# A selective scan on four engines: the state ring, the decays' lead and the order of the sums

## The chip, the cores and the metric

The kernel runs on one core of a Trainium2 chip. The core has five engines with an instruction queue each: PE (TensorE, matrix products), DVE (VectorE) and POOL (GpSimd) for elementwise work, ACT (ScalarE) for functions such as exp, and SP, which here only issues DMAs. The queues run side by side; an instruction that needs another engine's result waits for a semaphore, and everything behind it in its own queue waits with it. The metric is the device time of one execution in microseconds (us); lower is better.

## What is computed

Four sequences of 256 tokens with 512 features pass through two layers. The first is a layer norm with latent attention and a gated feed-forward beside it. The second is a layer norm with a selective state space block and a routed low-rank feed-forward beside it. The change concerns the state space block. Its core, cut from the reference:

```python
proj = hidden_states @ in_proj_w
x, z = jnp.split(proj, 2, axis=-1)
...
xc = jax.nn.silu(xc)                    
ssm_p = jnp.einsum('bdl,ed->ble', xc, x_proj_w)
...
def step(h, inp):
    x_t, dt_t, B_t, C_t = inp
    dA = jnp.exp(dt_t[..., None] * A)
    dBx = dt_t[..., None] * B_t[:, None, :] * x_t[..., None]
    h = dA * h + dBx
    y = jnp.einsum('bdn,bn->bd', h, C_t)
    return (h, y)
...
y = (ys + D_param[None, :, None] * xc) * jax.nn.silu(z)
return jnp.einsum('bdl,hd->blh', y, out_proj_w)
```

There are 1024 channels (d) and 16 states (n) for each of the four sequences (b), and the recurrence runs over 256 steps. All data is float32.

## The kernel before

The order of all work is written out by hand: each engine's queue holds its instructions in the order in which the program calls the helpers.

**Units.** The scan is cut into 128 units u = 0 to 127. Each sequence (called batch here) has PER = 32 of them: 8 columns c of 128 channels, each with NU = 4 groups g of four states. Unit u belongs to batch u // 32, column u % 32 // 4 and group u % 4. In a unit's tile of 128 x 1024 elements, the partitions hold 32 channels for each of four states, and the row holds four blocks of 256 time steps.

A unit passes through these steps:

- *spread* (line 937), once a column: four DMAs on SP each bring dt and dt*x of the column into the unit layout, as dts and dus (two tiles each).
- *decays* (971): four exponentials on ACT, line 982, exp(dt * A), into a decay tile. The first column of each block stays 0, so that one scan runs over all four blocks. From unit 4 on there are three decay tiles, used in turn.
- *scan_in* (986): from unit 8 on a no-op on DVE (989) that takes over two waits of what follows, for the decays of u and for the product with C of u-2. Then bx = B * (dt*x) into a PSUM tile on DVE (993).
- *scan* (998): the recurrence h = decay * h + bx along the row on DVE (1008), into one of two h tiles, and then the product hc = h * C on POOL (1013), into one of three hc tiles. Units 0 to 3 take tiles that other work lends (the table `lent`).
- *states_sum* (1019): four small matmuls on PE (1025) with the matrix `stack` add the four states of each channel into the PSUM tile ysum, over the four units of a column. For the first group a matmul with a diagonal matrix (1023) goes ahead: it starts ysum with D * x.
- *take_sum* (1028): ACT copies ysum away when a column is done (1030). The next column's line 1023 has to wait for that.

**The loop over units** (1384) issues, pass by pass: take_sum of a column whose last unit was u-2; decays of u+2; the work that the tables put here; scan_in(u); scan(u); gates; states_sum(u-1). The tables `at`, `mid_at`, `late_at` and `end_at` hold all else, by batch and unit: while batch b is scanned, the layer norm of batch b+1, its input projection (px, pz), its convolution (conv_in, conv_taps; dg, tap and xc on ACT, products with px on PE, some sums on POOL), its silu (conv_silu, unit 16 or 17), the projection to dt, B and C (pp_mm, units 17 and 18) and the step sizes (step_in, step_exp, step_out, step_x, from unit 21 on) are made, and the output of batch b-1 (out_mm, dense, expert_out). In the last batch only output remains beside the scan.

The first units also overlap the end of the first layer: its last matmuls fill PE up to unit 3, and the act pool, from which the h tiles and two of the decay tiles come, is opened after unit 2 in memory that these matmuls still read.

The few lines that matter most for the change:

```python
            da = decay[(u - 4) % 3]
...
            for n in (("da", u), ("hc", u - 2)):
                tc.add_manual_dep(i.ins, made[n].ins.name, early, reason="the scan's waits")
...
            h = act.tile([P, NG, S], F32, tag="h", name="h", bufs=2)
            hc = act.tile([P, NG, S], F32, tag="hc", name="hc", bufs=3)
...
        if 1 <= u <= total:
            states_sum(u - 1)
```

## Time and profile before

| | us |
|---|---|
| median of three runs | 840.59 (839.35 to 841.75) |
| the profiled execution | 840.18 |
| its span, first to last instruction | 838.4 |
| first bx of the scan starts at | 327.4 |
| last bx starts at | 826.5 |
| busy over the span: PE, DVE, ACT, POOL | 750.9, 654.6, 554.2, 496.9 |

Times in a trace are counted from the start of the span. In the tables of groups a row reads: line, engine, operation, output and inputs by the program's names, shapes and count, then the busy time and the mean of one in ns, then the time that the engine stood idle just ahead of these instructions, with what ended most of it. A row of the waits says which instruction of an engine waited for what, how long in all, how often, and the longest. A row of the timeline has the start, the duration, the engine, the line and the operation, and in brackets the idle time before. PE is drawn as busy from the start of a matmul to a modelled end, so its share says less than that of the others. The engine that a wait is put down to is the one whose semaphore came last by the trace; where that engine had long been done, it was another.

The steps of a unit in this trace: bx 1.23 us and scan 2.29 us on DVE, four exponentials in 1.7 us on ACT, the product with C in 2.36 us on POOL, the sum over states in 0.64 us on PE.

## The change

Five things are changed.

1. POOL writes the product with C over h itself. The separate hc tiles are gone; there are four h tiles in place of two h and three hc tiles.
2. There are four decay tiles in turn, and the decays of a unit are issued three passes ahead, not two; for the first unit of a batch it stays two. (`due` lists which decays a pass issues; pass 3 issues those of units 5 and 6.)
3. The no-op ahead of bx waits for more: the decays of u, the product of u-4, the sum of u-4, and, for the first unit of a column, the four DMAs of dus.
4. The sums over states are issued two units at a time, after each even pass: those of u-2 and u-1.
5. The lent tiles of units 0 to 3 follow from that: no hc, and h of unit 1 lies where lw lay.

```diff
-        for i in range(NG):
-            nc.sync.dma_start(t[i * NB : (i + 1) * NB], src)
+        made[n, b, c] = [nc.sync.dma_start(t[i * NB : (i + 1) * NB], src) for i in range(NG)]
...
-    lent = {
-        "d": ("d", "w_in", "d", "w_in"), "h": ("w_in", "u", "e", "u"),
-        "hc": ("w_in", "lw", "w_in", "lw"),
-    }
+    lent = {"d": ("d", "w_in", "d", "w_in"), "h": ("w_in", "lw", "e", "u")}
+    ahead = 3
...
-            da = decay[(u - 4) % 3]
+            da = decay[(u - 4) % (ahead + 1)]
...
-            for n in (("da", u), ("hc", u - 2)):
-                tc.add_manual_dep(i.ins, made[n].ins.name, early, reason="the scan's waits")
+            first = made["du", b, c] if g == 0 else []
+            for j in (*first, made["da", u], made["hc", u - 4], made["sum", u - 4]):
+                tc.add_manual_dep(i.ins, j.ins.name, early, reason="the scan's waits")
...
-            h, hc = lend("h", u), lend("hc", u)
+            h = lend("h", u)
         else:
-            h = act.tile([P, NG, S], F32, tag="h", name="h", bufs=2)
-            hc = act.tile([P, NG, S], F32, tag="hc", name="hc", bufs=3)
+            h = act.tile([P, NG, S], F32, tag="h", name="h", bufs=4)
...
-                hc[:, n], h[:, n],
+                h[:, n], h[:, n],
                 crows[b][:, g, :].unsqueeze(1).to_broadcast([P, NG // parts, S]), ALU.mult,
             )
-        live["hc", u] = hc
+        live["hc", u] = h
...
-            mm(ysum[k * NB : (k + 1) * NB, :], lhsT=stack, rhs=hc[:, k, :],
-               start=False, stop=(g == NU - 1))
+            made["sum", u] = mm(ysum[k * NB : (k + 1) * NB, :], lhsT=stack, rhs=hc[:, k, :],
+                                start=False, stop=(g == NU - 1))
...
-        decay_tile(act)
-        decay_tile(act)
+        for _ in range(ahead):
+            decay_tile(act)
...
+    due = {}
+    for v in range(5, total):
+        due.setdefault(max(v - ahead + (v % PER == 0), 3), []).append(v)
...
-        if 3 <= u < total - 2:
-            decays(u + 2)
+        for v in due.get(u, ()):
+            decays(v)
...
-        if 1 <= u <= total:
+        if u and u % 2 == 0:
+            states_sum(u - 2)
             states_sum(u - 1)
```

## What is predicted, and how

> **What bounds the kernel now.** I read the shares of the page first, then the waits of VectorE (DVE) over the scans, then a table of stretches, and last the timeline of all engines around the largest waits.

> ```profile
> L1008 DVE TENSOR_TENSOR_SCAN h<-decay,bx 128x1024 f32<-128x1024 f32 (+1 forms) x129 | 288.1, 2235 | 8.5 <-PE po L469 3.6
> L993 DVE TENSOR_TENSOR bx<-brow,dus 128x1024 f32<-128x1024 f32 x128 | 157.7, 1232 | 24.2 <-ACT decay L982 9.3
> ```

> The 128 units of the scan run one after another on DVE: bx, then scan. In the timeline two bx starts that nothing disturbs lie 3.585 us apart, so 128 units are 459 us, the largest single part of the 838.4 us span. The second number group is the prize: DVE stood still 24.2 us before bx. From unit 8 on, the waits are these (stretch 364 to 828 us):

> ```profile
> DVE bx L993 <- ACT decay L982: 9.3, 8, 4.1
> DVE bx L993 <- POOL hc L1013: 6.7, 10, 1.1
> DVE bx L993 <- ACT pad L771: 3.2, 1, 3.2
> DVE bx L993 <- DMA dus<-dud: 0.4, 2, 0.2
> DVE bx L993 <- DVE h L1008: 0.4, 2, 0.2
> ```

> With 0.3 us on a smaller row of POOL that is 20.3 us. The 3.2 us put down to ACT are really POOL's: that bx (unit 16) waits for hc of unit 14, which ended at 398.97, a quarter of a us before bx started at 399.22. So 20.3 us is the ceiling: 840.2 - 20.3 = 819.9. But who else is full while DVE waits?

> ```profile
> core 0: us, PE busy (x) PEld busy (x) DVE busy (x) ACT busy (x) POOL busy (x), PEclk, DMA share, GB/s
> 357.00:408.00 51.00, 48.76 (x284) 33.90 (x284) 43.36 (x25) 48.04 (x116) 44.37 (x30) 0.97 0.43 114
> 482.00:535.00 53.00, 49.08 (x271) 30.54 (x270) 50.11 (x30) 47.43 (x110) 49.76 (x32) 1.00 0.47 135
> 716.00:825.00 109.00, 85.63 (x391) 32.83 (x390) 106.37 (x61) 70.08 (x150) 86.11 (x46) 0.89 0.32 87
> ```

> In the last batch DVE alone is full. In the first, where the next batch's convolution is prepared beside the scan (357 to 408 us), PE is busy 48.8 of 51 us and ACT 48.0, and DVE only 43.4: there DVE's waits show that others can't follow. The end of this stretch on PE:

> ```profile
> 407.31 0.64 PE L1025 MATMUL ysum<-hc,stack 128*32 128x256 f32 x8
> 411.86 5.35 PE L833 MATMUL pp<-xc,xpw 128*64 128x256 f32 x16 [3.91 <-ACT xc L822]
> 417.14 0.64 PE L1025 MATMUL ysum<-hc,stack 128*32 128x256 f32 x8
> ```

> The first row is the sum of unit 16, the last that of unit 17; between them PE waits for the silu on ACT and makes both halves of pp. The bx of unit 20 started at 415.79. Keep these four times.

> [...] the no-op of scan_in with one or two waits leaves the pitch at 3.585 us. [...] after 3.91 us idle the 16 records of pp took 5.35 us, in the third batch 8 of them 1.94.

> **The change, part by part.**

> *Product over h.* POOL's instruction keeps its shape; I take the measured 2.36 us again (no row shows it in place; 0.05 us either way over 127 units would be 6 us of POOL, which idles before hc for 80.5 us in all and hides it; without that cover it would show only where POOL is late, some 1 us). The ring changes: before, the scan of u waits for POOL's product u-2, and that for PE's sum u-5 or earlier. Now bx of u waits for PE's sum of u-4. POOL's waits (6.7 + 0.3 + 3.2 = 10.2 us) go, for a product four units back ended 7.2 us or more before every bx. PE takes POOL's place.

> *Sums by two.* An odd unit is summed where it was, an even one a pass later, behind all that PE was given for that pass. PE's work is the same (0.57 us a sum), but bx of an even unit v+4 now needs a sum that stands where the sum of v+1 started. I compared those two starts for each even v. The slack is 1.6 us or more nearly everywhere, 3 to 5 in the last batch; it is short or negative at v = 8 (-0.8), 16 (-1.35: the four times above), 48 (-2.3), 52 (-0.7), 80 (-0.7), 82 (+0.8), 84 (-1.5). In return take_sum lies a pass before the next column's first sum; PE's wait for it (9.3 us, eight times) goes.

> *Decays three ahead.* ACT runs 4 exponentials (1.6 us) a unit; each is done a unit, 3.6 us, earlier for DVE. All eight waits (9.3 us) fit into that; the longest, 4.12 at unit 58, leaves nothing or half a us at unit 59. The dts that they read is there: SP issues it once the decays two columns before are done, and those too are a unit earlier. The price: one more group goes into ACT's queue at the start. At 353.18 ACT goes from the decays of 6 straight to a table load and the gate; now the decays of 7 stand ahead, their tile is new and waits for nothing, and ACT is busy without a gap of 0.2 us until 402.99. So all that it does up to there comes 1.6 to 1.7 us later. Queued behind are the layer norm, its transposes on PE and the convolution. The SP queue keeps its order.

> *DMA waits moved to the no-op.* Four bx at the first unit of a column, with five waits each, are 0.2 us late (the last two rows above): 0.8 us gained at most. If an added wait cost one semaphore event (50 ns on DVE's queue) each time, 120 units would lose 6 us; a first unit with five waits in bx still shows a 3.59 pitch elsewhere (unit 36), so I take 0.

> **The sum for the first batch**, with the order of the new program and the durations above. ACT's convolution weights, 374.64 before, come at 376.3, PE's product with them at 376.8. The sums of 8 and 9 stand behind two such products and a px: 376.8 + 1.85 + 1.75 + 1.8 + 1.2 = 383.4 for unit 8. Without it bx of 12 would run at 378.7 (before: 379.73). Onwards in the same way, PE and ACT by turns: sum 12 at 400.3, so bx 16 at 400.3 (before 399.22); sums 14 and 15 at 407.9 and 408.5 (before 405.8: 1.7 from ACT and 1.2 of sums moved behind a wait). Then take_sum, one group of decays, two xc, table, silu: 6 us on ACT, as before, to 414.5; PE has stood 5 us and makes pp in 5.35, to 419.9; sum 16 ends at 421.0. So bx of 20 starts at 421.0, not 415.79: **5.2 us lost** there, although six waits of before (8.6 us) are gone by name. DMA isn't the limit: by POOL's queue its dus lands near 415.

> **After it**, each stretch falls back on DVE's pace (PE waits for products again at units 23 to 29), so only differences count. Unit 29: +0.8. Second batch: 2.4 up to unit 51; pp starts at 532.2 instead of 537.3, being free of the sum ahead of it, and sum 48 ends at 539.2, so bx 52 keeps 1.2; the norm's wait of 0.74 goes, +2.0; then 4.1 and 0.8 at units 58 and 61, +6.9, of which 0.5 may be lost because dus of the third batch follows POOL and lands near 585: +6.4. Third batch: 2.1 up to unit 83; there PE has no lead, sum 80 ends at 664.2 (bx 84: +0.7) and sum 84 at 679.9 (bx 88: -0.2); the router's 0.8 and POOL's 0.8 then go: +1.4. Last batch: +0.7. The tail isn't touched. Together 0.8 + 6.4 + 1.4 + 0.7 - 5.2 = **4.1 us**. The profiled execution was 840.18 us for its span of 838.4; less 4.1 it is 836.1. The median of the runs is 840.59: **836.5**.

> **Rivals.**

> *A. As worked out: PE's sums stop bx in the first batch, the rest gains.* 836.5; 832 to 840 with the first batch's loss between 2 and 7.

> *B. PE isn't in the way.* If silu comes 2 to 3 us sooner and pp runs warm (3.9 instead of 5.35), bx 20 is no later than before and the first batch gains some: 840.6 - 9.3 - (2 to 11) = 820 to 829. For it: PE idles 3.91 us there. Against: that idling hangs on ACT, which has no gap.

> *C. Slower: the sum before the silu's pp stops DVE in every batch.* Place: bx of units 52 and 84, as at 20. It decides when PE or ACT enter the conv stretch of batches 2 and 3 late by the 1.7 us[...]: 5 us each instead of a gain of 2. 840.6 + 5.2 + 10 - 7.4 (the waits at units 29, 58, 61, 89, 93) = 848. For it: the two stretches have PE busy 93 to 95%. Against: ACT idles 1 to 2.4 us several times there (waiting for px and pdt), which swallows the extra group.

> *D. A with a larger loss at 20 or less from unit 58*: the two cancel, 838 to 843.

> **How the numbers follow.** A 0.48, B 0.17, C 0.20, D 0.15. A measurement of this kernel can tell about 0.3% (2.5 us) from no change: faster is below 838.1, slower above 843.1. A gives 0.42 of its 0.48 to faster, the rest to same; B all to faster; D 0.03, 0.09 and 0.03; C all to slower: 0.62, 0.15, 0.23. The range takes in A, D, the near half of B and of C, and the unknown 6 us of an added wait only in part: 826 to 846. A's own is 832 to 840.

> **What would show it.** In the new profile: bx waits for PE ysum, longest before unit 20 (5 us or more) and unit 12 (4 to 5), and hardly for POOL or decay; ACT's gap after unit 15's sum unchanged; pp again with a wait of 4 to 5 us in the first batch and shorter in the second; the wait of 4.12 gone; a pitch of 3.585 in undisturbed units. Wrong would be: a bx of unit 20 earlier relative to the end of the first layer's matmuls (B), long PE waits in batches 2 and 3 (C), or a pitch above 3.6.

## The result, and the profile after

| | before | changed |
|---|---|---|
| median, 22 runs each | 841.25 (838.04 to 842.88) | 839.27 (836.50 to 841.01) |
| ratio, 95% interval | | 0.9974 (0.9963 to 0.9986) |
| the profiled execution | 840.18 | 840.51 |
| its span | 838.4 | 838.7 |
| mean clock of PE in it | 0.953 | 0.931 |

The changed kernel is 0.26% faster: 2 us, where 4 were forecast. Its 22 runs lie in two groups, nine up to 837.4 us and nine from 840.4 on, with four between, and the profiled execution is one of the second. So its trace shows no gain over the trace of before; what follows is about where time moved between the two, and its losses are those of the slower group.

The groups of the changed kernel's page (line, engine, operation, tiles, count; busy time and mean ns; idle time ahead, with what ended most of it):

```profile
L1005 DVE TENSOR_TENSOR_SCAN h<-decay,bx 128x1024 f32<-128x1024 f32 (+1 forms) x129 | 288.1, 2235 | 8.1 <-PE po L469 3.3
L991 DVE TENSOR_TENSOR bx<-brow,dus 128x1024 f32<-128x1024 f32 x128 | 157.7, 1232 | 26.4 <-DMA bw<-in_base 6.6
```

The work of DVE is the same to a tenth of a us. Its idle time before bx has grown from 24.2 to 26.4 us. The waits in the scans (364 to 828 us: what bx waited for, us in total, times, longest):

```profile
DVE bx L991 <- DMA bw<-in_base: 6.6, 1, 6.6
DVE bx L991 <- ACT dg L776: 4.6, 1, 4.6
DVE bx L991 <- PE ysum L1022: 4.1, 3, 2.1
DVE bx L991 <- ACT decay L979: 3.5, 3, 2.7
DVE bx L991 <- ACT pad L771: 2.7, 1, 2.7
```

POOL's waits are gone, and of the decays' 9.3 us 3.5 are left, 2.7 of them in name only. In their place stand five single waits in the first batch, before units 8 (2.74 us), 10 (1.64), 12 (2.66), 16 (4.58) and 20 (6.61). The names on the largest are wrong: a weight transfer named bw has nothing to do with bx, and bx of unit 20 started at 425.16, a quarter of a us after the sum of unit 16 ended on PE at 424.90. Each of the five starts 0.2 to 0.3 us after the end of the sum that it needs. All five wait for PE.

Two of the stretches of before (start and end, length, busy time of each engine with its count, PE's clock, DMA share, GB/s):

```profile
core 0: us, PE busy (x) PEld busy (x) DVE busy (x) ACT busy (x) POOL busy (x), PEclk, DMA share, GB/s
357.00:408.00 51.00, 44.82 (x235) 33.28 (x236) 38.57 (x23) 47.32 (x110) 40.44 (x27) 0.87 0.41 104
482.00:535.00 53.00, 49.92 (x280) 32.65 (x279) 51.99 (x32) 48.31 (x119) 48.78 (x32) 1.00 0.49 130
```

In the first stretch DVE got through 38.6 us of work, before 43.4. If PE's work had been the bound there, PE would be busier than before. It is less busy, 44.8 us, before 48.8, with 235 matmul records where there were 284, and its clock is 0.87, before 0.97. PE does less and does it more slowly. In the second stretch DVE is now nearly full (52.0 of 53 us, before 50.1).

What PE waited for between 357 and 430 us, first before, then with the change (engine, output, line, what it waited for; us, times, longest):

```profile
PE pp L833 <- ACT xc L822: 3.9, 1, 3.9
PE pt L743 <- ACT xnt L735: 1.9, 1, 1.9
PE px L806 <- ACT dg L776: 1.0, 1, 1.0
PE px L806 <- ACT xc L784: 0.5, 1, 0.5
PE px L759 <- ACT sz L956: 0.3, 1, 0.3
```

```profile
PE pp L833 <- ACT xc L822: 4.9, 1, 4.9
PE pt L743 <- ACT xnt L735: 3.5, 1, 3.5
PE px L806 <- ACT xc L784: 2.0, 1, 2.0
PE pdt L872 <- ACT dt L878: 1.8, 1, 1.8
PE px L806 <- ACT dg L776: 0.9, 1, 0.9
```

Together 7.6 us before and 13.1 after. PE waits for ACT where it did and longer, and at one place more (pdt). The places on PE's timeline (start, duration, engine, line, operation, count, idle time before), first the beginning before the change, then with it:

```profile
357.25 1.82 PE L743 MATMUL pt<-cst,xnt 128*128 128x128 f32 x8 [1.92 <-ACT xnt L735]
359.86 1.08 PE L1025 MATMUL ysum<-hc,stack 128*32 128x256 f32 x8
360.99 1.21 PE L872 MATMUL pdt<-nrm,dtw 32*128 32x256 f32 x4
```

```profile
358.46 1.97 PE L743 MATMUL pt<-cst,xnt 128*128 128x128 f32 x8 [3.52 <-ACT xnt L735]
362.20 2.07 PE L872 MATMUL pdt<-nrm,dtw 32*128 32x256 f32 x4 [1.76 <-ACT dt L878]
364.20 1.22 PE L1020 MATMUL ysum<-xc,dgs 128*128 128x256 f32 x2
365.35 1.94 PE L1022 MATMUL ysum<-h,stack 128*32 128x256 f32 x16
...
397.49 2.74 PE L806 MATMUL px<-pad,dg 128*128 128x256 f32 x8 [2.02 <-ACT xc L784]
400.02 2.88 PE L759 MATMUL px<-xn1T,w_in 128*128 128x256 f32 x8
...
417.68 6.03 PE L833 MATMUL pp<-xc,xpw 128*64 128x256 f32 x16 [4.91 <-ACT xc L822]
423.63 0.70 PE L1020 MATMUL ysum<-xc,dgs 128*128 128x256 f32 x2
424.26 1.07 PE L1022 MATMUL ysum<-h,stack 128*32 128x256 f32 x16
```

Read the first four rows of the changed kernel in order. Before, the sum of unit 4 stood between pt and the second pdt: PE had it to do while ACT made dt, and pdt then took 1.21 us. Now that sum stands behind pdt. PE stands 1.76 us with nothing it may do, runs pdt in 2.07, and makes two sums in 1.94 that take 1.07 us elsewhere (last row). The moved sum is late by the wait, and by the slower clock there (0.50 from 357.64 to 367.86, next table). The last three rows are the largest case: pp waits 4.91 us, takes 6.03, and both sums stand behind it.

How slow PE runs can be read from the clock that it was granted. The columns are those of the stretches above, PE's clock is the third number from the end; the first row is of the kernel before, the others of the changed one:

```profile
361.22:367.86 6.64, 6.64 (x40) 4.65 (x41) 6.44 (x4) 6.61 (x16) 4.91 (x3) 1.00 0.97 240
```

```profile
357.64:367.86 10.22, 7.63 (x32) 4.38 (x33) 7.18 (x5) 10.22 (x25) 6.75 (x4) 0.50 0.57 143
395.18:398.58 3.40, 1.38 (x7) 0.98 (x6) 3.33 (x3) 3.40 (x11) 1.04 (x2) 1.00 0.68 128
398.60:402.00 3.40, 3.40 (x10) 2.69 (x9) 0.98 (x1) 3.37 (x10) 3.24 (x4) 0.50 0.00 0
```

Before, PE was at half clock (0.50) for 3.4 us after its wait for xnt (357.8 to 361.2), had no gap after it and was back at full clock (1.00). With the change it stays at half clock for 10.2 us, and the new wait before pdt lies in that time. Most of the px product and of the next one falls into a second stretch at half clock, 398.6 to 402.0; before, the clock was 1.00 from 361.3 to 412.4.

To separate stages I take the lead of each bx: its start in the trace of before less its start here. A change of the lead between two units is gained or lost there, wherever the first layer ended.

| stretch (units) | change of the lead predicted | measured |
|---|---|---|
| first batch, 4 to 20 | -5.2 | -9.4 |
| 20 to 24 | none | -0.6 |
| 24 to 32 | +0.8 | +0.8 |
| second batch, 32 to 64 | +6.4 | +7.3 |
| third batch, 64 to 96 | +1.4 | +1.2 |
| last, 96 to 127 | +0.7 | +0.5 |

After unit 24 the sum was 9.3 and is 9.8. The first batch was to cost 5.2 and costs 10.0.

## The experiments

Three theories stood at the start. Theory M: in the first batch both queues that were changed cost time, the sums moved behind PE's waits and the extra group of decays on ACT, and PE runs slowly after the new waits (pdt took 2.07 us there, before 1.21). R1: the ring of four tiles is too short for sums by two at all. R2: only the extra group on ACT costs, the pairs are harmless.

All kernels are the changed one with the lines shown. The first two columns of numbers are changes of the lead between units in one profiled execution each, the last two are the timed runs against the kernel before.

| sums; decays ahead | units 4 to 24 | 24 to 127 | median us | ratio (95%) |
|---|---|---|---|---|
| changed kernel: pairs; three | -10.0 | +9.8 | 839.27 | 0.9963 to 0.9986 |
| single; three | -0.4 | +3.7 | 836.63 | 0.9933 to 0.9957 |
| pairs; two | -7.4 | +6.7 | 840.38 | 0.9977 to 0.9998 |
| single, pairs from pass 25; three | -1.9 | +9.7 | 832.21 | 0.9880 to 0.9909 |
| single, pairs from 25; two, three from unit 24 | +0.2 | +10.0 | 830.26 | 0.9860 to 0.9885 |
| pairs; two up to unit 7, then three | -9.5 | +9.1 | 839.72 | 0.9975 to 1.0002 |
| single; two | +0.1 | +0.4 | 838.54 | 0.9966 to 0.9987 |
| as the 830.26, no DMA waits in the no-op | 0.0 | +7.7 | 830.98 | 0.9872 to 0.9909 |
| pairs, unit 16 alone; three | -3.6 | +9.2 | 833.47 | 0.9902 to 0.9938 |
| as the 830.26, 48, 49, 80, 81 alone | +0.2 | +3.4 | 834.64 | 0.9917 to 0.9944 |
| even sums at the head of the pass; three | -6.1 | +8.8 | 834.85 | 0.9909 to 0.9955 |
| the same; two, three from unit 24 | -1.2 | +9.8 | 830.28 | 0.9855 to 0.9887 |

The second and fourth row are the same program up to pass 24 and show -0.4 and -1.9: so much do two profiled executions differ, and smaller differences in these columns are not read. PE's clock goes with it: from the wait for xnt on it was at half for 6.8 us in the second (355.0 to 361.9) and for 10.2 in the fourth (357.4 to 367.7).

**Single sums.**

```diff
-        if u and u % 2 == 0:
-            states_sum(u - 2)
+        if 1 <= u <= total:
             states_sum(u - 1)
```

> The changed kernel with the sums issued one unit a pass, as before; the rest of the change stays. In the profile of the changed kernel bx of unit 20 starts 9.4 us later than before, and the waits for PE's sums of units 4, 6, 8, 12 and 16 make up all of it. Theory M (even sums stand behind a pass of convolution on PE, and one more group of decays stands at the head of ACT's queue): without the pairing the waits at units 8, 10 and 12 go, bx 20 comes at 411 to 415 and bx 21, which needs the sum behind pp, at about 419.5, so the first batch costs nothing against before; the later gain shrinks from 9.8 to 7 to 9, since ysum waits for take_sum again. 831 to 834 where before is 841. Rival R1 (the ring of four tiles itself is too short, whatever the order): bx 20 stays 5 us or more late, time 836 or more. Rival R2 (ACT's extra group alone): bx 20 stays 7 us or more late, time 838 or more.

836.63 us. The loss of the first batch is all but gone, and so are 6 us of the later gain, where 1 to 3 were expected. The time alone would fit R1; but bx of unit 20 came at 414.08, not 5 us late, so in the first batch the ring isn't what costs. The extra group on ACT is still there; R2 falls. The pairs, the part that costs most in the first batch, are also worth most after it.

**Decays two ahead, pairs kept.**

```diff
-        due.setdefault(max(v - ahead + (v % PER == 0), 3), []).append(v)
+        due.setdefault(max(v - 2, 3), []).append(v)
```

> The changed kernel with the decays issued two passes ahead everywhere, as before; four decay tiles, pairs of sums and the ring of four stay. Theory M: the table load, layer norm and convolution on ACT stand 1.7 us earlier, so the first batch loses 9.4 less 2 to 3, about 7; but the waits for decays return later (4.1 at unit 58 and some smaller, about 6), so 841 to 844. R1: bx 20 is late by 9 as in the changed kernel, time 844 to 847. R2: bx 20 is back at 416 to 418, time 836 to 839.

840.38 us, just below what theory M gave. The pairs alone lose 7.4 us by unit 24; the group alone lost 0.4 to 1.9 in the run before and in the next; both together 10.0. To the accuracy of two profiles the two add. Three units ahead is worth 9.8 - 6.7 = 3.1 us after the first batch.

**Single sums in the first batch alone, then also decays two ahead there.**

```diff
-        if u and u % 2 == 0:
+        if 1 <= u <= 24:
+            states_sum(u - 1)
+        elif u > 24 and u % 2 == 0:
             states_sum(u - 2)
             states_sum(u - 1)
```

> The changed kernel with single sums up to pass 24 and pairs from there on. Theory M: bx 20 at 411 to 415 and bx 21 at about 419.5, the first batch even with before, and the whole later gain of 9.8 kept: 830 to 832. R1: 836 or more. R2: 838 or more, as bx 20 stays 7 us late.

```diff
-        due.setdefault(max(v - ahead + (v % PER == 0), 3), []).append(v)
+        due.setdefault(max(v - (ahead if v >= 24 and v % PER else 2), 3), []).append(v)
```

> The changed kernel with single sums up to pass 24 and the decays two ahead up to unit 23; from there on as changed. Only the ring of four h tiles with the product written over h, the fourth decay tile and the no-op's waits then act in the first batch. Theory M: the first batch is even or gains up to 3 us (its queues on PE and ACT are those of before, and POOL's waits are gone): 828 to 831. R1: bx 20 stays 5 us late: 836. R2 expects 829 too; it parts from M by the run with single sums first alone.

832.21 and 830.26 us: 1.05% and 1.3% faster than before (the intervals are in the table). The ring of four tiles with pairs from pass 25 keeps the whole later gain, so R1 falls as well. With both delays undone in the first batch, all five of PE's waits of before, 357 to 430 us, are back to the tenth of a us, and one more of 1.3 us (pcr for dt, line 859) stands beside them. The pt row is 1.9 again and not the 3.5 of the changed kernel, and the new pdt row is gone.

**Where the extra group stands.** Before or behind the layer norm on ACT?

```diff
-        due.setdefault(max(v - ahead + (v % PER == 0), 3), []).append(v)
+        due.setdefault(max(v - (ahead if v >= 8 and v % PER else 2), 3), []).append(v)
```

> The changed kernel, but the decays go three units ahead only from unit 8 on, so that the decays of 7 are issued in pass 5 and the layer norm comes ahead of the extra group on ACT. The changed kernel loses 10.0 us between the bx of unit 4 and that of unit 24, 7.4 with the pairs alone and 1.9 with the extra group alone. Theory that both delays add and that the pairs carry most of it (PE's sums moved behind PE's waits): the loss is 7.5 to 9 us and the time 837 to 839, since the group still enters before the convolution's products. Rival, that only the group's place ahead of the layer norm costs: loss 7.5, time 836.5. Rival, that the place doesn't matter and only the number of groups does: loss 10, time as the changed kernel, 839.5.

839.72 us and 9.5 lost: what was expected if the place doesn't matter, within the accuracy of a profile. In the trace pt waits 1.92 us again, but the second pdt now waits 3.62 where it waited 1.76: 5.5 and 5.3 us together. The group has only moved PE's wait from one product to the next; PE is at half clock for 10.2 us here too (358.0 to 368.3).

**The ring alone.** Single sums and decays two ahead everywhere (the first two diffs of this section together).

> The changed kernel with single sums and decays two ahead everywhere; left of the change are the product written over h, the ring of four state tiles, the fourth decay tile and the waits in the no-op. Theory that the gain of the change comes from the decays three ahead and the pairs in the later batches, and that the ring alone takes POOL's waits away only to put others in their place: 837 to 840. Rival, that the ring is the gain and the other two parts only cost: 832 or less. Rival, that a ring of four is too short even for single sums: 842 or more.

838.54 us. Its waits of DVE from 364 to 828 us:

```profile
DVE bx L991 <- ACT decay L979: 17.4, 9, 4.0
DVE bx L991 <- POOL xc L813: 1.3, 1, 1.3
```

Before, POOL and the decays together made 6.7 + 9.3 us, and 3.2 more belonged to POOL. With POOL's product out of the way the decays take its place nearly us for us: 17.4. Each of the nine bx starts 0.12 us after its own decays ended, so here the name is right. A bound taken away alone handed its waits to the next; it takes three units ahead to get them: with the same single sums they bring the later gain from 0.4 to 3.7 us.

**The DMA waits in the no-op.**

```diff
-            first = made["du", b, c] if g == 0 else []
+            first = []
```

> The best version so far (830.26: single sums and decays two ahead in the first batch, pairs and three ahead after it), without the four waits for dt*x moved to the no-op, so that bx itself waits for them at the first unit of each column. If a bx with many waits starts late only where one of them isn't met yet, 830 to 832. If each of the 32 first units paid 0.2 us, as the four waits of the kernel before that were put down to a DMA, 836.

830.98 us, with 830.26 for the same kernel with these waits; the two intervals overlap, and 6 us is excluded. The traces show the first reading at work: bx of units 16 and 20, whose decays come late, start 0.32 and 0.31 us after these decays ended, and 0.12 us with the waits in the no-op, while first units that wait for nothing keep the pitch (3.59 us, units 12, 24 and 28 among them). One thing isn't explained: in the table the later gain is 7.7 here against 10.0. That lies almost wholly at units 52, 56, 88 and 100, each 0.5 to 0.8 us later than in the other kernel, and is more than the timed runs show (0.7 us).

**The sum of unit 16 put back ahead of pp.**

```diff
-        if u and u % 2 == 0:
+        if u in (17, 18):
+            states_sum(u - 1)
+        elif u and u % 2 == 0:
```

> The changed kernel with one sum put back: that of unit 16 is made in pass 17 again, ahead of PE's product pp, all other pairs as they are. The bx of unit 20 waited 6.61 us for this sum in the changed kernel, which ended at 424.80. Theory that PE's whole stretch is late and the one sum only the place where it shows: bx of unit 21, whose sum of 17 stands behind pp as before, then sets the time, at about 424.8; the loss from unit 4 to unit 24 falls from 10.0 to 5.5 to 6 us and the time is 835 to 836.5. If instead the next sum in the queue takes over nearly all of the wait, the loss stays above 8 us and the time above 838.

833.47 us: 5.8 us from one sum's place by the medians, more than either expectation; against the faster group of the changed kernel's runs (about 837.2) it is 3.8. PE's timeline, the rows that answer to those of the changed kernel:

```profile
396.35 2.00 PE L806 MATMUL px<-pad,dg 128*128 128x256 f32 x8 [2.05 <-ACT xc L784]
398.18 1.89 PE L759 MATMUL px<-xn1T,w_in 128*128 128x256 f32 x8
...
414.85 5.35 PE L833 MATMUL pp<-xc,xpw 128*64 128x256 f32 x16 [3.91 <-ACT xc L822]
420.13 0.64 PE L1022 MATMUL ysum<-h,stack 128*32 128x256 f32 x8
```

The place of the wait moved as the theory said: bx of unit 21 now waits (1.66 us) for the last row, the sum of unit 17 behind pp. It started at 420.97; the trace stood 1.74 us further ahead at unit 4, so that is 422.7 on the changed kernel's clock. There, bx of 20 started at 425.16 and that of 21 one pitch (3.59) later, at 428.75. The 6.0 us between are three things: one pitch, because unit 20 was done while PE was busy with pp (3.59); pp 0.7 us shorter, with 0.7 less between its end and the bx (the column's D product, 0.7 in the changed kernel, no longer lies there); and 1.1 us that PE was earlier at pp's start. The expectation of 424.8 had left out the last two. The 1.1 is no effect of the edit, since it lies ahead of pass 17: px ran faster in this execution (2.00 us, as before at clock 1.00; 2.74 in the changed kernel), after as long a wait. The stretch with the wait, with the columns of above:

```profile
394.62:398.01 3.39, 1.66 (x8) 1.48 (x9) 3.32 (x3) 3.39 (x11) 1.16 (x2) 1.00 0.52 94
```

No half clock follows it here; the next one begins at 415.1.

**Later batches: pp behind a sum again.**

```diff
-        if u and u % 2 == 0:
+        if 1 <= u <= 24 or u in (49, 50, 81, 82):
+            states_sum(u - 1)
+        elif u > 24 and u % 2 == 0:
```

> The best version so far (830.26), with the sums of units 48, 49, 80 and 81 made singly as well, so that PE's product pp of the second and third batch again stands behind the sum of unit 48 or 80. The prediction had said that the pairs bring the second batch forward because pp is then free of the sum ahead of it. If so, the wait comes back before unit 53 and 85 (1 and 1.6 us in the version with single sums everywhere) in exchange for the 2.06 before unit 84: 830.5 to 832. If pairs gain elsewhere in the later batches (ACT's copy of the column's sum), these four change nothing but the 2.06 us: 828 to 829.

834.64 us, 4.4 more than with pairs (6.6 by the leads of the two profiled executions). The direction is that of the first expectation, the size isn't. PE's timeline in this kernel, then in the one with pairs from pass 25:

```profile
533.05 1.22 PE L1020 MATMUL ysum<-xc,dgs 128*128 128x256 f32 x2 [3.40 <-ACT xc L1027]
534.20 1.08 PE L1022 MATMUL ysum<-h,stack 128*32 128x256 f32 x8
535.22 3.61 PE L833 MATMUL pp<-xc,xpw 128*64 128x256 f32 x8
```

```profile
530.70 1.94 PE L833 MATMUL pp<-xc,xpw 128*64 128x256 f32 x8 [1.24 <-ACT xc L822]
533.62 1.94 PE L833 MATMUL pp<-xc,xpw 128*64 128x256 f32 x8
```

The first sum of a column must wait until ACT has copied the former column's sum out (the bracket in the first row: 3.40 us). With single sums pp stands behind that wait and starts 4.5 us later, and its first half takes 3.61 us, not 1.94. In pairs the column's sum is copied out a pass before the next one starts. So the later gain of the pairs is this: of the 6 us between 3.7 and 9.8, four sums account for all (3.4 against 10.0). The timed runs agree: single sums everywhere after the first batch cost 836.63 - 832.21 = 4.4 us, these four alone 834.64 - 830.26 = 4.4.

**Even sums at the head of the pass.** PE gets as many sums in a pass as in the kernel before, and the column's copy keeps its distance.

```diff
+        if u and u % 2 == 0:
+            states_sum(u - 2)
         for v in due.get(u, ()):
...
         if u and u % 2 == 0:
-            states_sum(u - 2)
             states_sum(u - 1)
```

> The changed kernel, with only the place of the even units' sums moved: each stands at the head of its pass, ahead of that pass's work for PE, and the odd unit's sum at the end as in the change. PE gets as many sums in each pass as in the kernel before. If the loss of the changed kernel in the first batch is the queue's (sums moved behind products that wait for ACT), it falls from 10.0 us to about that of the extra group alone, 2 to 3.5, and with most of the later gain of 9.8 kept the time is 831.5 to 834. If the loss is due to the ring of four or to PE's load as such, the time stays above 837.

The second kernel has the decays two ahead up to unit 23 as well.

> As the run with the even units' sums at the head of the pass, and the decays only two units ahead up to unit 23. If the two delays of the first batch still add, 1.5 to 2 us less than that run: 829.5 to 832.5, about the best version so far. If the decays of the first batch are no longer in the way once PE's queue is in order, no difference between the two.

834.85 and 830.28 us. The second is what was expected; the first lost more than expected, and its trace says where:

```profile
414.49 3.67 PE L833 MATMUL pp<-xc,xpw 128*64 128x256 f32 x8 [4.91 <-ACT xc L822]
418.10 1.22 PE L1020 MATMUL ysum<-xc,dgs 128*128 128x256 f32 x2
419.25 0.84 PE L1022 MATMUL ysum<-h,stack 128*32 128x256 f32 x8
420.02 1.94 PE L833 MATMUL pp<-xc,xpw 128*64 128x256 f32 x8
```

The sum of unit 16 (third row) stands between the two halves of pp: the first half is issued in pass 17, the second in pass 18. It still waited for silu, and bx of 20 started at 420.36, a quarter of a us after it, with a wait of 8.15 us. With decays two ahead silu ends 4.5 us earlier and bx of 20 starts 5.0 us earlier, both counted from the bx of unit 4. It starts at 416.72, by the same count 1.35 us behind the kernel of 830.26 (415.44), where it waits not for a sum but for its own decays, which stand behind silu on ACT. So the extra group costs 5 us here, where it cost 0.4 to 1.9 with single sums, whose bx of 20 needs no sum from behind silu's product, and 2.6 with pairs. Why 5 and not 2.6 isn't shown.

## Why the prediction was wrong

Right by its own steps:

- The place: bx waits for PE's sums, longest before unit 20; POOL's waits are gone, and so is the decay wait of 4.12 us. (Unit 12, where 4 to 5 us were expected, shows 2.66; units 16 and 8 show more.) The pitch of undisturbed units is 3.59 us still, with more waits in the no-op (also at first units of a column, such as unit 36), so the added waits cost nothing that shows, as was taken. The product in place has a median of 2.36 us, as hc had.
- The extra group on ACT: the gate's table load came at 354.39, 1.2 us later than before (1.6 to 1.7 predicted), and the convolution later in turn.
- Everything after unit 24: 9.8 us measured, 9.3 predicted, each batch within 1 us. The step "pp is free of the sum ahead of it" carried it: pp waited 1.24 us there and each half took 1.94, where before the sum ahead of it had waited 3.07 us for ACT and the half took 2.62. Putting that sum back cost 4.4 us.

Wrong: the sum for the first batch, 5.2 us lost by unit 20; measured 9.4, and 10.0 by unit 24. The step that failed is "1.7 from ACT and 1.2 of sums moved behind a wait". By its own times (405.8 to 408.5; the two terms would make 2.9) it put the sum of unit 15, and silu behind it, 2.7 us late. Both came 5.8 us late: the sum ended at 411.64, silu at 417.62 (414.5 predicted). What followed held: 6.0 us from that sum to silu's end, and from pp's end to the sum that bx of 20 needs 1.2 us, for which 1.1 had been taken.

Which of the two terms was too small can be read from the runs. The end of silu on ACT, counted from the bx of unit 4 so that the first layer drops out:

| kernel | silu ends, us (on the clock of before) |
|---|---|
| before | 411.8 |
| ring alone; also the 830.26 kernel | 411.8 |
| the extra group alone (two executions) | 413.4, 414.9 |
| pairs alone | 415.0 |
| changed: both | 417.7 |

The group was put at 1.7 us and cost 1.6 to 3.1; the moved sums were put at 1.2 and cost 3.2. Behind both stands "PE's work is the same (0.57 us a sum)", with the durations of before taken for it. The work is the same; the time is not, for two reasons that the traces show:

- Sums 4 and 5 behind the second pdt weren't in the list of short slacks at all, as the slack of unit 4 is above 1.6 us, and cost 2.74 us before unit 8. The sum had been what PE did while ACT made dt; now PE waits 1.76 us there, and pdt, both sums and part of px follow at half clock (0.50 up to 367.9).
- The clock: half (0.50) for 10.2 us from the first wait on, before 3.4, and 3.4 us more at px. ACT's lateness and PE's fed each other: bx of 12 came at 385.26 (383.4 predicted), bx of 16 at 404.15 (400.3).

A second term was mis-sized in the same way: pp was put at the 5.35 us of before; after the wait of 4.91 us it took 6.03, with the clock at 0.60 over these 6.03 us (0.68 over the 5.35 of before).

3.1 for the late silu, 0.7 for pp, and 0.1 and a quarter of a us from pp's end to the bx make the 4.2 us between 421.0 and 425.16. The late silu is by far the largest, and it is a chain of small waits.

Of the rivals, D ("A with a larger loss at 20") is what happened, with its 838 to 843 around 839.27; A had the right mechanism and the wrong size. C's place, the second and third batch, shows 2.08 us before unit 84 and nothing before 52, and falls. B wanted silu 2 to 3 us earlier and pp at full clock; no kernel shows that, not even the one of 830.26: silu ends as before there, and pp took 5.35 us after a wait of 3.9.

One thing stays open: why the changed kernel's own runs fall in two groups 3.3 us apart. The nine of the lower group lie about 837.2 us, 4 us below the median of before, which is the size that was forecast; how much the first batch lost in them no trace shows, so the 10.0 us hold for the execution that was traced. In those runs, too, the pairs of the first batch cost: single sums there gave 832.21, 5.0 us less. The kernel with all of the change but pairs and decays doesn't show the two groups (15 of its 22 runs lie between 838.2 and 839.0). PE's mean clock is 0.941 to 0.947 in the nine lower runs and 0.931 to 0.943 in the nine upper ones. PE's clock came out differently after the waits of 2.02 and 2.05 us ahead of px, in two traces of kernels with the same program up to there (last section); that this makes the two groups is the author's guess, not shown.

## What to carry to other kernels

Before a small operation is moved later in an engine's queue to save a wait elsewhere, look at what the engine does in its place: if it was filling the time of a wait, the move costs that wait, and here PE was also at half clock for 10.2 us where it had been for 3.4. Take such a change stage by stage; here the sums by two gain 4 us in the later batches and lose 7 in the first (timed runs), and keeping them to where they gain gave 832.21 us instead of 839.27, with the decays treated alike 830.26. And when a wait is taken away, count what was due just behind it: the ring of tiles alone removed POOL's waits and got back nearly as much from the decays.
